# Graph message passing on one core: the last gather of three pairs of groups in four replaced by copied columns of x

## The chip, the cores and the metric

The kernel runs on one core of a Trainium2 chip. The metric is the device time of one execution in microseconds (us). Engines are named as in the profile: PE is the matrix engine (PEld its weight loads), DVE the vector engine, ACT the scalar engine, POOL the general engine that also issues the gathers, SP the engine that issues most of the plain transfers. Each engine runs its own instruction stream in order; streams meet only through semaphores. An engine's sequencer reads the stream, does register work itself and passes the other instructions to the engine.

## The reference

There are 12,500 nodes with 96 features each (x) and 412,500 edges, sorted by their target node. For every edge the reference computes a message, and for every node it sums the messages:

```python
def _mlp(h, W, b, gamma, beta):
    h = relu(h @ W + b)
    mu, var = mean(h, axis=0), mean(square(h - mu), axis=0)
    return gamma * (h - mu) * rsqrt(var + EPS) + beta

node_feat = _mlp(x, W_node, ...)
edge_feat = _mlp(edge_attr, W_edge, ...)            # 4 attributes per edge
message = concatenate([x[row], x[col], edge_feat], axis=1)
message = _mlp(message, W_msg, ...)                 # 288 -> 96
agg = segment_sum(message, col, num_segments=12500)
out = layernorm(x + agg + node_feat)
```

`row` is an edge's source (any node, in no order), `col` its target (sorted). So `x[row] @ W_msg[:96]` needs 412,500 rows from scattered places, and everything that depends on `col` lies in narrow windows.

## The kernel before, in words

The edges are cut into 3223 tiles of 128, four tiles make a group (806 groups), and four groups make a block. The kernel first computes the table `p_tab` = x times the first third of W_msg, and `q_tab` = x times the second third, and writes both to HBM (`tables`). A tile's source rows then come from `p_tab` by one indirect transfer of 128 rows, issued by POOL: `gather` (L207) issues one for each tile of a group, so four for a group. A pair of groups shares a buffer `pg` of [128, 2, 4, 96] floats.

Buffers: `ring` holds 7 such pairs (RING = 14 groups). The first 116 groups (SPILL) are gathered at once while other engines prepare tables and statistics; SP writes them from the ring to HBM (`spill`) and brings them back later (`blocks`, `fetch`, tile `pb`). Three of these groups take their last tile by single rows through SP instead (`EARLY`, `early_rows`). The other 690 groups, the late ones, are gathered during the main loop, `RING` groups ahead: `ahead_of(g)` issues the gathers of group g into the place that group g - RING has left. `plan` mixes early and late blocks into one order of 806 steps.

Before the loop lies a stage with the statistics of nodes (`nodes`) and edges (`edge_norm`). x transposed, [96, 12544], is loaded into the tile `big` (as `xp`) at the start; `nodes` overwrites it with the residual, multiplies that by `center` and stores the result in HBM (`y0_d`). In the loop, from step 64 on, `residual` loads it back into `big`, one part of 8 blocks every fourth step, for the output stage after the loop.

One step of the main loop handles one group. The order on POOL, SP, PE, DVE and ACT is the order of the program (`manual_schedule`). For step k:

- `message(k)`: DVE adds the gathered rows `pg` to the matmul result z and applies relu, giving h (L645).
- `squared` (ACT, every second step, L659) and `moments` (DVE, two adds, L665) for the variance.
- `places_of` (DVE, every fourth step, L653): the 0/1 matrix that sends edges to target nodes.
- `add` (DVE, every fourth step, L708 and L709): adds a block's sums to `agg` at a place that is read from memory into a register (L698).
- `sums(k - 2)` (PE, L689): h times the 0/1 matrix. `edges` (PE, L614) and `prepare` (ACT, L622) make the left operand of a later step.
- `linear(k + 2)` (PE, L628): z, four matmuls of [128 x 128] by [128 x 96].
- for a late group: `ahead_of`, the gathers for the group RING later.

For the groups of the first four blocks (RAW) the rows come from x itself, are transposed on PE and multiplied by W_msg (`transposed`, L633), since `p_tab` is not there yet.

Of the kernel before, what the change touches and what calls it, by code (L numbers as in the profile page):

```python
# [13 lines left out]
F32 = mybir.dt.float32  # L14
BF16 = mybir.dt.bfloat16
I32 = mybir.dt.int32
U8 = mybir.dt.uint8
# [9 lines left out]
P = 128  # L27
# [36 lines left out]
RING = 14  # L64
# [7 lines left out]
CL, CE = 3, 1  # L72
BUSY = 5
# [34 lines left out]
def gnn(ctx, tc, t):  # L108
# [8 lines left out]
    lin_d = dram.tile([len(FETCHED), P], I32, name="lin_d")  # L117
    stack_d = dram.tile([HI + PLACES * BG, RL], BF16, name="stack_d")
# [5 lines left out]
    rpool = ExitStack()  # L124
    nc.sync.dma_start(src_raw, t["src"][:, :RAW * BG * GT])
    ring = rpool.enter_context(tc.tile_pool(name="ring", bufs=RING // 2))
# [90 lines left out]
    def blocks():  # L217

        waiting = []
        for b in range(SPILL // BG + BEHIND):  # L220
            if b < SPILL // BG:
                for i in range(0, BG, 2):
                    pg = ring.tile([P, 2, GT, C], F32, name="pg")
# [45 lines left out]
    with tc.tile_pool(name="win", bufs=1) as win, tc.tile_pool(name="win_ps", bufs=2, space=PSUM) as ps:  # L269
# [8 lines left out]
        nc.sync.dma_start(lin_d, lins)  # L278
        by_block = "p (b g) t -> p b (g t)"
# [202 lines left out]

    order, steps = plan()

    def fast(ring):
        y0s, pair = [], [None]

        def ahead_of(g):
            if g % 2 == 0:
                pair[0] = ring.tile([P, 2, GT, C], F32, name="pg")  # L490
            if g < NG:
                return gather(g, pair[0][:, g % 2, :, :])

        with tc.manual_schedule(engines={ET.SP, ET.Pool}):
# [9 lines left out]
            with tc.tile_pool(name="nd", bufs=1) as nd, tc.tile_pool(name="nd_ps", bufs=2, space=PSUM) as nd_ps, \  # L504
                    tc.tile_pool(name="er", bufs=2) as er, tc.tile_pool(name="es", bufs=2) as es, \
                    tc.tile_pool(name="es1", bufs=1) as es1, tc.tile_pool(name="es_ps", bufs=3, space=PSUM) as es_ps:
                node, n, extra = nodes(nd, nd_ps), 7, early_rows(er)
                for i, _ in enumerate(edge_norm(es, es1, es_ps)):
                    next(node, None)
                    if i:  # L510
                        next(extra, None)
                    while 16 * i + 150 >= 20 * n:
                        next(store, None)
                        n += 1
                for x in (node, store, extra):
                    for _ in x:
                        pass
            got = {g: ahead_of(g) for g in range(SPILL, SPILL + RING)}
        with tc.tile_pool(name="fix", bufs=1) as fix, tc.tile_pool(name="msg", bufs=2) as work, \
# [75 lines left out]

            def transposed(k):
# [27 lines left out]
            def linear(k):  # L624
                s, g = steps[k]
                n = min(GT, NT - g * GT)
                for i in range(n):
# [3 lines left out]
                                     stop=g not in raw)  # L631
# [82 lines left out]
            with tc.manual_schedule(engines={ET.SP, ET.Pool, ET.PE, ET.DVE, ET.Activation}):  # L714
# [13 lines left out]
                for k in range(last):  # L728
# [33 lines left out]
                    if k >= 64 and k % 4 == 0 and loads:  # L762
                        y0s.append(residual(loads.pop(0)))
# [223 lines left out]
    y0s, bad = fast(ring)  # L987
# [5 lines left out]
    rpool.close()  # L993
# [60 lines left out]
```

## Time and profile before

| | |
|---|---|
| time, median of 3 runs | 4123.67 us (4118.46 to 4125.99) |
| profiled execution | 4123.06 us, span 4121.3 us |
| granted PE clock, mean | 0.675 |
| POOL busy | 3092.1 us (75%), of which gathers 3009.5 + 60.8 |
| DVE, ACT busy | 1584.5 us (38%), 1123.0 us (27%) |
| PE, PEld busy | 2632.2 us (64%), 2244.2 us (54%) |

A row of groups in the profile reads: line, engine, operation, what it writes and reads, shapes and count, then busy time in us and the mean duration in ns, then the idle time of the engine right before it and what ended that. A "q" behind an engine's name marks its sequencer. "issue" is time in which the engine waited for nothing that the profile shows.

### The profile page before, as it was taken

To read this page: it belongs to the slowest core of one execution; us is meant where nothing else is said; L and a number is where in the kernel's file an instruction comes from. 1 tells how busy PE (TensorE), PEld (TensorE's weight loads), DVE (VectorE), ACT (ScalarE), POOL (GpSimd) and SP (SyncE) were. 2 spreads that over 40 slices of the span, in tenths; PEclk is the share of its full clock that TensorE was granted. 3 is DMA by queue.
4 is the path that set the end of the run, shared out by engine and by line. 5 is a ranking of instruction groups with operands and counts; after the bars stand their busy time and mean duration, and the time that the engine had idled before them with its cause. 6 is when DMAs were issued, how large, how long until landed. Compare 5 with 4: busy or idle time off the path is not lost.

```text
span 4121.3 us, 43082 instructions
## 1 busy us (share of the span) xinstructions
PE 2632.2 (64%) x14949; PEld 2244.2 (54%) x15169; DVE 1584.5 (38%) x3051; ACT 1123.0 (27%) x1226; POOL 3092.1 (75%) x3248
## 2 busy tenths in 40 slices
PE   4256665666666666666666666666666666666667
PEld 3012324565666656556655566655565565666656
DVE  2499995333333233322333333333233333333323
ACT  1477882222222222212222222222122222222212
POOL 7777777777777777777777777777777777777774
PEclk7667886767766666656667666666666666666665
DMA  8855662223222222222222222222222222222222
GB/s 234 279 140 123 165 161 62 60 70 77 72 50 55 59 57 58 59 54 58 56 58 58 59 47 57 60 58 55 58 59 55 58 60 56 50 59 57 58 45 64
DMA packets 214865, 317.20 MB, mean 77 GB/s; under 512 B 126498, under 2 KB 132988, under 8 KB 211808
## 3 DMA queue, kind: packets, MB, share of 16 engines
q0 software_dynamic: 103040, 158.48, 19.2%
q1 hardware_dynamic: 98635, 150.92, 12.3%
q10 hardware_dynamic: 12960, 4.93, 0.5%
q8 instruction: 122, 2.00, 0.2%
q14 instruction: 108, 0.88, 0.1%
HBM read 258.19 MB, written 55.89 MB: 76 GB/s over the span
## 4 chain that ended last, share of the span: by engine, by line
POOL 50%; issue 22%; DVE 13%; DMA 10%; PE 4%; ACT 1%; SPq 0%; POOLq 0%; another core or an unknown queue 0%; DVEq 0%; ACTq 0%
POOL pg L207 50%; DMA pg<-p_tab,src 9%; DVE estats L419 9%; PE z L628 1%; PE py L971 1%; PE pa L689 1%; DVE mixed L665 1%; DMA x<-in_ea 0%; DVE part L424 0%; DVE h L645 0%; PE pn L358 0%; DVE nstats L360 0%; DVE big L369 0%; DVE y0s L388 0%; DVE agg L394 0%
## 5 line engine op out<-in xcount | busy, mean ns | idle before, releaser
L207 POOL DMA_INDIRECT pg<-p_tab,src x3156 | 3009.5, 954 | 964.7 <-issue 919.7
L628 PE MATMUL z<-rhs,left 128*128 128x96 f32 x6446 | 1276.3, 361 | 1099.9 <-DVE h L645 1092.3
L628 PEld LDWEIGHTS z<-rhs,left 128*128 128x128 f32 x6446 | 1166.7, 267 | 1304.9 <-DVE h L645 1271.9
L645 DVE CUSTOM_DVE_ANT_0 h<-z,pg 128x384 f32<-128x384 f32 x690 | 384.1, 557 | 2301.7 <-DMA pg<-p_tab,src 2244.6
L659 ACT ACTIVATE sq<-h 128x768 f32<-128x768 f32 x404 | 339.8, 841 | 2586.6 <-DVE h L645 2577.5
L689 PE MATMUL pa<-at,h 128*97 128x80 f32 x6446 | 940.5, 307 | 4.9 <-DVE h L645 4.9
L689 PEld LDWEIGHTS pa<-at,h 128*97 128x97 f32 x6446 | 889.4, 227 | 5.9 <-DVE h L645 5.9
L665 DVE TENSOR_TENSOR mixed<-mixed,sq 128x384 f32<-128x384 f32 x802 | 449.8, 561 | 13.9
L622 ACT ACTIVATE left<-pr 127x1024 f32<-127x1024 f32 x403 | 406.8, 1009 | 90.1 <-PE pr L614 60.8
L413 PE MATMUL pr<-ea,wide 128*128 128x512 bf16 x590 | 225.5, 476 | 213.7 <-ACT r L417 135.8
L419 DVE BATCH_NORM_STATS2 estats<-r 128x6 f32<-128x512 f32 x606 | 360.9, 676 | 0.0
L417 ACT ACTIVATE r<-pr 128x1024 f32<-128x1024 f32 x303 | 307.4, 1024 | 93.0 <-DVE estats L419 65.2
L413 PEld LDWEIGHTS <-wide 128*128 128x128 bf16 x606 | 68.8, 114 | 345.9 <-issue 326.1
L614 PE MATMUL pr<-late,we 128*128 128x512 bf16 x515 | 240.6, 530 | 19.2 <-DVE at L653 15.5
L653 DVE TENSOR_TENSOR at<-rel,mixed 128x496 f32<-128x496 bf16 x202 | 135.2, 669 | 6.8
L614 PEld LDWEIGHTS <-we 128*128 128x128 bf16 x806 | 108.4, 144 | 25.2 <-issue 24.7
L207 POOL DMA_INDIRECT pg<-in_x,src_raw x64 | 60.8, 950 | 20.7 <-issue 19.2
L386 PEld LDWEIGHTS pn<-center,big 96*128 96x128 f32 x196 | 42.4, 277 | 33.0 <-DVE y0s L388 22.9
L645 DVE CUSTOM_DVE_ANT_0 h<-z,pb 128x384 f32<-128x384 f32 x100 | 52.5, 548 | 13.6 <-PE z L628 13.5
L386 PE MATMUL pn<-center,big 96*128 96x96 f32 x196 | 41.9, 358 | 17.0 <-DVE y0s L388 16.3
L191 PE MATMUL pt<-w_msg,big 96*128 96x192 f32 x196 | 37.2, 357 | 17.2 <-ACT trow L195 11.7
L709 DVE TENSOR_TENSOR agg<-pa,agg 97x79 f32 x202 | 46.5, 230 | 0.0
(125 smaller groups left out, 658.2 us busy)
## 6 DMA issues: line engine op xcount, KB each, us to landing
pg<-p_tab,src POOLq DMA_INDIRECT x3156
pb<-spill SPq DMA_DIRECT2D x29, 768.0 KB
spill<-pg SPq DMA_DIRECT2D x55, 384.0 KB
ea<-stack_d SPq DMA_DIRECT2D x25, 480.0 KB
stack_d<-y SPq DMA_DIRECT2D x24, 448.0 KB
late<-stack_d SPq DMA_DIRECT2D x57, 180.0 KB
rhs<-q_tab SPq DMA_DIRECT2D x202, 46.5 KB
x<-in_ea SPq DMA_DIRECT2D x8, 896.0 KB
```

The source lines that it names most:

```text
L207: made = [nc.gpsimd.indirect_dma_start(out=pg[:, i, :], out_offset=None, in_=tab[:, :], in_offset=bass.IndirectOffsetOnAxis(ap=idx[:, i:i ...
L413: nc.tensor.matmul(pr[:, k % 2, :], wide[:, P * i:P * (i + 1)], ea[:, b % J, :], start=True, stop=True)
L417: nc.scalar.activation(r, pr, AF.Relu)
L419: nc.vector.bn_stats(stats[:, (k - o) % NS, (k - o) // NS, :], r[:, 1 - o, :])
L614: nc.tensor.matmul(prs[s, half][:, i, :], we[:, 2 * half + i, :], block[s], start=True, stop=True)
L622: nc.scalar.activation(x[:C + WN, 2 * half:2 * half + n, :], pr[:C + WN, :n, :], AF.Relu)
L628: nc.tensor.matmul(zb[k % ZB][:, i * C:(i + 1) * C], left[s % 2][:KR, g % BG, i * P:(i + 1) * P], rhs[:KR, s % RB, g % BG, :], start=True, ...
L645: nc.vector._custom_dve(TENSOR_ADD_SAT, out=h[:, :n, :], in0=z, in1=rows[:, :n, :], s0=MOST, s1=0.0)
L653: nc.vector.tensor_tensor(to, rel[:, b:b + m, :].unsqueeze(3).to_broadcast([P, m, GT, WN]), nodes_of[:, :m].unsqueeze(2).to_broadcast([P, ...
L659: nc.scalar.activation(sq[:, :m, :n, :], hb[k // 2 % HP][:, k % 2:k % 2 + m, :n, :C], AF.Square)
L665: nc.vector.tensor_tensor(wide_sq, wide_sq, sq[:, i, :, :], op=OP.add)
L689: nc.tensor.matmul(by_place[s % 2][:C + 1, :NW], hb[k // 2 % HP][:r, k % 2, t, :], at[s % AB][:r, i, o + NW * t:o + NW * (t + 1)], start=i ...
```

## The change

For 249 pairs of late groups (three pairs in four: `COPIED`) the second group issues three gathers instead of four. Its last tile of 128 edges gets its rows in another way: x transposed stands in `big` during the whole loop, one column for each node, and for each edge of the tile one column (96 partitions, four bytes) is copied into a tile `xc` of [96, 128]. `linear` then multiplies `xc` by the first third of W_msg and adds that to z; the ring's place of that tile is set to zero once, so that `message` adds nothing.

The copies are made by ACT and DVE, in portions of 32: each portion first loads 32 node numbers (times four, as byte addresses) from a small tile into 32 registers of the engine, then issues 32 copies, each from the address in one register. `SHARES` says how many of the 128 columns ACT copies (64, 64, 96 in turn); DVE copies the others. A `Stream` per engine issues at most one portion per step, at most 12 steps ahead of the use, with six `xc` tiles. SP brings the numbers for four pairs at a time (`listed`).

Around it: RING is 16; the ring is eight fixed tiles; x transposed is loaded a second time into `big` near the end of the edge statistics (`back`), after `nodes`, which now advances two steps at a time, has used it; the loads of the residual into `big` move behind the last copy; the scratch for the gathers' descriptors is 8192 instead of the default of 16384 bytes.

```diff
-RING = 14
+RING = 16
+XB = 6
+TURN = 4
+AT_A_TIME = 32
+SHARES = (64, 64, 96)
+AHEAD_BY = 12
+RATE = 0.36
+LP = (NG - SPILL) // 2
+COPIED = [q for q in range(RING // 2, LP - 6) if q % TURN != TURN - 1]
...
+        nc.sync.dma_start(cols, t["lasts"][1::2, :].rearrange("(p k) e -> p k e", k=4))
+        nc.vector.tensor_scalar(cols, cols, 4.0, None, op0=OP.mult)
+        nc.sync.dma_start(col_d.rearrange("(p k) e -> p k e", k=4), cols)
...
+    def back(i):
+        part = slice(i * P, min(i + CH // 2, NB) * P)
+        nc.sync.dma_start(xp[:, part], t["xp"][:, part])
...
         def ahead_of(g):
-            if g % 2 == 0:
-                pair[0] = ring.tile([P, 2, GT, C], F32, name="pg")
+            q = (g - SPILL) // 2
+            slot = ring[q % len(ring)]
+            without = int(g % 2 and q in COPIED)
+            if without and q % len(ring) not in zeroed:
+                zeroed.add(q % len(ring))
+                nc.vector.memset(slot[:, 1, GT - 1, :], 0.0)
             if g < NG:
-                return gather(g, pair[0][:, g % 2, :, :])
+                return gather(g, slot[:, g % 2, :, :], without)
...
+            def columns(j, lo, hi, engine):
+                q = COPIED[j]
+                to = xcs[j % XB].bitcast(U8)
+                _, val = nc.values_load_multi_w_load_instructions(
+                    numbers[q // TURN % 2][:, q % TURN, lo:hi], engines=[engine], min_val=0, max_val=4 * (N - 1),
+                    skip_runtime_bounds_check_because="they are nodes' numbers times four")
+                for i, x in enumerate(val):
+                    a, b = to[:, 4 * (lo + i):4 * (lo + i + 1)], places_in_x[:, bass.ds(x, 4)]
+                    if engine == ET.DVE:
+                        nc.vector.tensor_copy(a, b)
+                    else:
+                        nc.scalar.activation(a, b, AF.Copy)
+
+            class Stream:
+                def __init__(self, engine):
+                    self.engine, self.done, self.due = engine, 0, 0.0
+                    self.parts = [(j, o, o + AT_A_TIME) for j in range(len(COPIED)) for o in range(0, P, AT_A_TIME)
+                                  if (o < SHARES[j % len(SHARES)]) == (engine == ET.Activation)]
+                    self.per = RATE * len(self.parts) / len(COPIED)
+                def step(self, k):
+                    self.due = min(self.due + self.per, 1.5)
+                    while self.due >= 1 and self.done < len(self.parts):
+                        j, lo, hi = self.parts[self.done]
+                        if COPIED[j] // TURN > loaded[-1] or uses[COPIED[j]] - k > AHEAD_BY or \
+                                (j >= XB and uses[COPIED[j - XB]] >= k):
+                            break
+                        columns(j, lo, hi, self.engine)
+                        self.due -= 1
+                        self.done += 1
...
+                    if i == GT - 1 and copied:
+                        nc.tensor.matmul(zb[k % ZB][:, i * C:(i + 1) * C], xcs[COPIED.index(q) % XB],
+                                         w_msg[:, 0, :], start=False, stop=True)
...
-                    if k >= 64 and k % 4 == 0 and loads:
+                    listed()
+                    for x in streams:
+                        x.step(k)
+                    if all(x.done == len(x.parts) for x in streams) and loads:
                         y0s.append(residual(loads.pop(0)))
...
-    nc = bacc.Bacc("TRN2", target_bir_lowering=False, num_devices=1)
+    nc = bacc.Bacc("TRN2", target_bir_lowering=False, num_devices=1, dynamic_dma_scratch_size=8192)
```

More of the change, by code (lines that the diff above doesn't have):

```diff
@@ L123, in gnn @@
     src = const.tile([P, 2, CW], I32, name="src")
-    rpool = ExitStack()
     nc.sync.dma_start(src_raw, t["src"][:, :RAW * BG * GT])
-    ring = rpool.enter_context(tc.tile_pool(name="ring", bufs=RING // 2))
+    ring = [const.tile([P, 2, GT, C], F32, name=f"pg{i}") for i in range(RING // 2)]
     xp = big[:C]
@@ L596, in transposed @@
+            streams = [Stream(e) for e in (ET.Activation, ET.DVE)]
             def transposed(k):
@@ L625, in linear @@
                 s, g = steps[k]
+                q = (g - SPILL) // 2
+                copied = g >= SPILL and g % 2 and q in COPIED
                 n = min(GT, NT - g * GT)
@@ L992, in gnn @@
         output(y0s, "win")
-    rpool.close()
 def kernel(**inputs):
```

38 lines of the change are left out of this document (32 added, 6 removed).

## The prediction, made blind

> **What bounds the kernel now.** I read the page's busy shares and chain of waits first, then the groups, the windows by stage, the timeline of the slowest engine and the waits.
>
> ```profile
> span 4121.3 us, 43082 instructions
> PE 2632.2 (64%) x14949; PEld 2244.2 (54%) x15169; DVE 1584.5 (38%) x3051; ACT 1123.0 (27%) x1226; POOL 3092.1 (75%) x3248
> POOL 50%; issue 22%; DVE 13%; DMA 10%; PE 4%; ACT 1%; SPq 0%; POOLq 0%; another core or an unknown queue 0%; DVEq 0%; ACTq 0%
> L207 POOL DMA_INDIRECT pg<-p_tab,src x3156 | 3009.5, 954 | 964.7 <-issue 919.7
> ```
>
> POOL heads the chain with 50%, and the 22% of "issue" are the pauses between its gathers: 919.7 us over 3156 gathers, 0.29 us each. The timeline shows the beat, and the windows show that it never stops (columns: window, length, then busy us and count for PE, PEld, DVE, ACT, POOL).
>
> ```profile
> 4005.14 0.94 POOL L207 DMA_INDIRECT pg<-p_tab,src  x1 [0.30 <-issue]
> 4006.39 0.95 POOL L207 DMA_INDIRECT pg<-p_tab,src  x1 [0.30 <-issue]
> ...
> 200.00:650.00 450.00, 254.90 (x794) 105.70 (x810) 442.79 (x706) 321.90 (x316) 341.09 (x358) 0.73 0.57 141
> 650.00:2350.00 1700.00, 1131.54 (x7036) 1026.88 (x7142) 528.90 (x1127) 372.33 (x417) 1285.36 (x1361) 0.68 0.27 60
> 2350.00:4057.00 1707.00, 1128.80 (x6654) 1019.22 (x6752) 514.07 (x1097) 350.91 (x397) 1290.77 (x1367) 0.66 0.25 56
> ```
>
> One gather starts every 1.25 us (1700 / 1361 = 1.249, 1707 / 1367 = 1.249; 450 / 358 = 1.257 before the loop). From about 650 us to 4057 us, the loop, the kernel is a line of gathers with everything else waiting for it:
>
> ```profile
> ACT sq L659 <- DVE h L645: 2577.5, 395, 12.4
> DVE h L645 <- DMA pg<-p_tab,src: 2244.6, 617, 8.6
> PE z L628 <- DVE h L645: 1092.3, 470, 7.4
> ```
>
> In those 3407 us DVE is busy for 528.9 + 514.1 = 1043 us and ACT for 372.3 + 350.9 = 723 us. This idle time is what the change spends.
>
> **What the change removes.** `COPIED` holds q from 8 to 338 without every fourth: 249 pairs, one gather less each. 249 x 1.25 = 311 us. In the loop POOL then needs 3407 - 311 = 3096 us. That part is certain; whether anybody can use it depends on who replaces the gathers.
>
> **What it adds.** 249 x 128 = 31,872 copies of one column of x. By `SHARES`, ACT gets 18,592 of them, 581 portions of 32, and DVE 13,280, 415 portions. Each portion is one register load of 32 numbers, and then 32 copies, each with its own address, so a register instruction goes before each. The copies exist nowhere in the trace; their parts do.
>
> The register load has these rows (1 number L715, 8 numbers L572 and L698, 16 numbers L457; min/median/max in ns):
>
> ```profile
> L715 ACTq TENSOR_LOAD <-flag x1: 473/473/473, 641.1 to 641.1; - x1
> L698 DVEq TENSOR_LOAD <-base_at x26: 541/598/612, 678.9 to 4059.2; - x26
> L572 SPq TENSOR_LOAD <-base_at x26: 708/776/806, 655.4 to 3959.9; - x26
> L457 SPq TENSOR_LOAD <-elin x24: 1165/1226/2637, 225.2 to 598.5; - x24
> ```
>
> From 8 to 16 numbers SP's load grows by 450 ns, 56 ns a number. For 24 numbers more than 8 that is 1.35 us: 0.60 + 1.35 = 1.95 us on DVE, 0.47 + 1.35 = 1.8 us on ACT. Ends: 0.5 us if a load of 32 costs what a short one does, 2.45 us at twice the row of 16. I take the middle, since the only step seen between two sizes lies there.
>
> One copy on DVE:
>
> ```profile
> 2153.38 0.16 DVE L708 TENSOR_TENSOR total<-pa,total 97x1 f32<-97x1 f32 x1
> 2153.52 0.24 DVE L709 TENSOR_TENSOR agg<-pa,agg 97x79 f32 x1
> ...
> 2173.36 0.15 DVE L708 TENSOR_TENSOR total<-pa,total 97x1 f32<-97x1 f32 x1
> 2173.43 0.23 DVE L709 TENSOR_TENSOR agg<-pa,agg 97x79 f32 x1
> ...
> L709 DVEq FUSED_REGOPS  x202: 69/69/79, 679.7 to 4063.3; - x101
> L461 SPq MOVE erow<-p_tab x384: 29/29/38, 226.4 to 604.9; - x192
> ```
>
> L709 is the one instruction here with a register for an address. It starts 0.14 us after L708 when the address is worked out between the two (at 2153, behind a load) and 0.07 us when that was done before (at 2173). Its register instruction makes two addresses in 0.069 us; one addition lies nearer the 0.03 of a MOVE. So 0.14 - 0.07 + 0.04 = 0.11 us a copy, between 0.07 and 0.15. A DVE portion: 1.95 + 32 x 0.11 = 5.5 us; 415 of them are 2283 us.
>
> One copy on ACT:
>
> ```profile
> 179.37 1.04 ACT L337 ACTIVATE z<-rlin 128x1024 bf16<-128x1024 f32 x1
> 180.31 1.04 ACT L339 ACTIVATE z<-rlin 128x1024 bf16<-128x1024 f32 x1
> 181.26 1.04 ACT L338 ACTIVATE rlin<-rlin 128x1024 f32<-128x1024 f32 x1
> ...
> L659 ACT ACTIVATE sq<-h 128x768 f32<-128x768 f32 x404 | 339.8, 841 | 2586.6 <-DVE h L645 2577.5 <-DVE h L643 5.5 <-POOL squares L679 3.6
> L310 ACT ACTIVATE y<-x 128x1792 bf16<-128x1792 f32 x8 | 13.5, 1694 | 9.1 <-DVE x L309 8.7 <-DMA x<-in_ea 0.4
> ```
>
> Between 768 and 1792 elements the duration grows by (1694 - 841) / 1024 = 0.83 ns an element, so 201 ns are fixed. Back to back, 1024 elements start every 0.945 us, of which 0.853 are elements: 0.09 us fixed. Four bytes then cost 0.09 to 0.10 us if the next overlaps and 0.20 us if nothing does. The register instruction runs on the sequencer while the engine works on the copy before. I take 0.10. An ACT portion: 1.8 + 32 x 0.10 = 5.0 us; 581 of them are 2905 us.
>
> **What hides what.** A load occupies the sequencer, not the engine, so it can run while the engine works on what was queued before:
>
> ```profile
> L708 DVE TENSOR_TENSOR total<-pa,total 97x1 f32<-97x1 f32 x202 | 30.5, 151 | 4.0 <-PE pa L785 3.0 <-DVE h L645 0.3
> L645 DVE CUSTOM_DVE_ANT_0 h<-z,pg 128x384 f32<-128x384 f32 x690 | 384.1, 557 | 2301.7 <-DMA pg<-p_tab,src 2244.6 <-PE z L628 34.3 <-remote 22.7
> L665 DVE TENSOR_TENSOR mixed<-mixed,sq 128x384 f32<-128x384 f32 x802 | 449.8, 561 | 13.9
> ```
>
> The 26 loads of L698 stand right before L708, and L708 has 4.0 us of idle time in all, not 26 x 0.6. In each step a portion follows h (0.56 us) or the second half of the moments (0.56): 0.5 us of a DVE load is covered, 415 x 0.5 = 208. On ACT it follows sq or left (723 us over about 807 instructions, 0.9 each): 0.85 x 581 = 494. In the loop:
>
> - POOL 3096.
> - DVE 1043 + 2283 - 208 = 3118.
> - ACT 723 + 2905 - 494 = 3134.
>
> Three engines within 40 us of each other. The longest, ACT, saves 3407 - 3134 = 273 us, not 311. Streams that are level also wait for each other: sq waits for h, the moments for sq, h for a gather, and a ring place comes free only after h. The ring of 16 groups holds some 70 us of gathers (16 groups of 3.64 at 1.25 us), so only part is lost; I put 25 us on it, under 1% of the loop.
>
> POOL may itself slow down. A gather that starts while DVE holds both its SBUF inputs is stretched; one that has long started isn't:
>
> ```profile
> 103.15 2.03 DVE L309 TENSOR_TENSOR x<-x,y 128x1792 f32<-128x1792 f32 x1 [7.65 <-ACT y L308]
> 104.04 1.95 POOL L207 DMA_INDIRECT pg<-p_tab,src  x1 [0.30 <-issue]
> ...
> 8.28 0.94 POOL L207 DMA_INDIRECT pg<-in_x,src_raw  x1 [0.30 <-issue]
> 8.79 0.20 DVE L153 TENSOR_SCALAR center<-ident 96x96 f32<-96x96 f32 x1
> ```
>
> The first gather ends 0.82 us after L309 does (105.99 against 105.18), so only the first 0.13 us of a gather needs what DVE held. A copy in flight there costs at most a copy's time. About 2478 gathers are left in the loop; with 0.11 us at most, half of it on average, and DVE copying for 1460 of 3118 us: 2478 x 0.055 x 0.47 = 64 us, and 0 if a copy of four bytes doesn't hold it. With 30 POOL has 3126 us, still level, so it changes nothing in the longest.
>
> On that port the Trainium skill goes further (SBUF — State Buffer, Who interferes with whom): a copy within SBUF may run in a two-port mode, and whoever has the shared pair second is blocked for the whole instruction. L153, a one-source DVE instruction within SBUF, left its gather at 0.94 us, which speaks against a full block; if each copy did block, it is the fifth case below.
>
> **The smaller edits.** The second matmul of each copied tile (249) costs PE 0.36 us by L628's mean, 90 us in all; the 1092 us in which PE waits for h cover it:
>
> ```profile
> L628 PE MATMUL z<-rhs,left 128*128 128x96 f32 x6446 | 1276.3, 361 | 1099.9 <-DVE h L645 1092.3
> big<-in_xp SPq DMA_DIRECT2D x14, 336.0 KB
> big<-y_d SPq DMA_DIRECT2D x12, 384.0 KB
> SPq L578 <- PE z L628: 2914.6, 195, 20.5
> ```
>
> `back` loads xp a second time: 14 loads, 4.8 MB, at the 141 GB/s of the window 200:650 some 34 us of transfers. On SP they pass the edge blocks and the spill stores; POOL doesn't wait there and DVE, 98% busy, sets that stage, so 0, up to 34 if the blocks come late. Running the nodes two steps at a time only moves work within a stage that DVE fills anyway. The residual loads move to the last steps, behind the last copies: 4.8 MB where DMA is a quarter busy. SP has 2915 us of waiting; a late one would hold the output, which reads them in order: 0, up to 10. The list of numbers (2 KB every four pairs) rides on the same SP idle time; if it is late, the register load waits and with it all behind it on ACT and DVE, sq and h first. Ring 16 adds one pair of lead. The descriptor scratch is halved; no row shows a gather waiting for room there (the pauses are a constant 0.30), so 0.
>
> **The sum**, against the profiled execution (4123.06 us for a span of 4121.3; the median of the runs is 0.6 above): 4123 - 273 + 25 + 5 (half of the residual's bound) = 3880 us.
>
> **The rivals.**
>
> - *POOL stays alone the bound* (copies cheaper: a load nearer 1 us or DVE near 0.07). 4123 - 311 = 3812, with the stretch of gathers up to 3850. For it: both copies were priced above their lower ends. Against: the loads have a row at 16 numbers, 1.23 us. Chance 0.27.
> - *The forecast*, three engines level, 3850 to 3960. Chance 0.38.
> - *ACT or DVE dearer by a few per cent*, 3960 to 4115: each 0.005 us on ACT's copy adds 581 x 32 x 0.005 = 93 us. Chance 0.10, and 0.04 for the strip around no change.
> - *Slower: ACT's copies set the pace.* It decides where an ACT portion passes (3407 - 723 + 494) / 581 = 5.47 us, a copy of 0.115. At 0.12 a portion is 5.64, ACT needs 3277 + 229 = 3506, and the time is 4123 + 99 = 4222; at 0.13 it is 4408. For it: the register instruction and the copy share one sequencer, of which no ACT row shows the rate. Against: DVE's rows give 0.11 for both together. Chance 0.16.
> - *Slower: every DVE copy blocks POOL.* 13,280 x 0.07 = 930 us on POOL: 3812 + 930 = 4742. L153 speaks against it. Chance 0.05.
>
> **Range and chances.** 3815 to 4280: below lies little but the bare 3812; above, ACT at 0.123 and more, and the blocked POOL, about 0.15 together. The forecast's own range is 3850 to 3960. Under 0.2% (8 us) a measurement of this kernel cannot tell from no change. Faster 0.27 + 0.38 + 0.10 = 0.75, same 0.04, slower 0.16 + 0.05 = 0.21.
>
> **What would show it.** 2907 gathers from p_tab in place of 3156, plus 64 from x; still 1.25 us apart if POOL keeps its pace, with gaps that end on DVE h where it doesn't. Register loads of 32 near 1.8 to 1.95 us, copies every 0.10 and 0.11 us. ACT's wait for h down from 2577 us, DVE's for pg from 2245, both to a few hundred at most. The forecast is wrong if one of the three engines still waits for a thousand microseconds, or if gathers last beyond 0.95 us throughout.

## The result, and the profile after

The changed kernel takes 4069.51 us in the median (4068.61 to 4070.25), the kernel before, beside it, 4121.07. The ratio is 0.988, with a 95% interval of 0.985 to 0.992: faster by 1.2%, where the prediction said 3880 us, ratio 0.94. Beside each set of runs below the kernel before was timed again, and it takes 4103 to 4121 us in some sets and 5091 to 5199 in others, so each run is compared with the kernel before of its own set.

The page of the changed kernel, its head, the chain of waits and the groups that answer to those shown of before:

```profile
span 4067.6 us, 109367 instructions
PE 2517.9 (62%) x15667; PEld 2155.1 (53%) x15667; DVE 3005.8 (74%) x16338; ACT 2936.1 (72%) x19818; POOL 2853.5 (70%) x2999
...
DVE 28%; issue 24%; ACT 16%; POOL 8%; DMA 7%; DVEq 6%; PE 5%; ACTq 5%; SPq 1%; POOLq 0%
```

```profile
L215 POOL DMA_INDIRECT pg<-p_tab,src x2907 | 2770.4, 953 | 1166.0 <-issue 779.0 <-DVE h L733 250.4 <-DMA spill<-pg 46.8
L653 ACT ACTIVATE xc<-big 96x4 uint8 x18592 | 1863.5, 190 | 589.8 <-issue 569.8 <-PE pr L697 1.7 <-DMA late<-stack_d 1.3
L651 DVE COPY xc<-big 96x4 uint8 x13280 | 1460.9, 196 | 711.2 <-issue 707.5 <-DMA late<-stack_d 2.1
```

POOL led the chain with 50% and now has 8%. Its 2907 gathers still last 0.953 us in the mean, but POOL now stands idle 250 us for h: h frees a ring place, and h is late. DVE and ACT carry the chain, with their loads (DVEq 6%, ACTq 5%). The waits turned round as well:

```profile
POOL pg L215 <- DVE h L733: 250.4, 90, 15.1
ACT sq L747 <- DVE h L733: 151.5, 92, 4.0
DVE h L733 <- PE z L713: 52.7, 23, 7.6
DVE mixed L753 <- ACT sq L747: 51.0, 38, 2.5
```

ACT's wait for h fell from 2577 to 151 us, and DVE's wait for gathers is gone.

Where the time went is read from three rows of each kernel: the edge statistics (the stage before the loop), h (its first start opens the loop) and the gathers (the last start ends it). The columns are min/median/max in ns, then first and last start in us. Before, then after:

```profile
L419 DVE BATCH_NORM_STATS2 estats<-r x606: 633/676/695, 215.4 to 621.5; 128x6 f32<-128x512 f32 x152
L645 DVE CUSTOM_DVE_ANT_0 h<-z,pg x690: 457/557/559, 665.3 to 4059.2; 128x384 f32<-128x384 f32 x173
L207 POOL DMA_INDIRECT pg<-p_tab,src x3156: 940/945/4104, 83.4 to 4056.4; - x198
```

```profile
L431 DVE BATCH_NORM_STATS2 estats<-r x606: 626/676/696, 227.8 to 665.7; 128x6 f32<-128x512 f32 x152
L733 DVE CUSTOM_DVE_ANT_0 h<-z,pg x690: 458/557/561, 709.6 to 4022.0; 128x384 f32<-128x384 f32 x173
L215 POOL DMA_INDIRECT pg<-p_tab,src x2907: 938/944/3408, 84.0 to 4019.2; - x194
```

| part | before, us | after, us | difference |
|---|---|---|---|
| until the first h | 665.3 | 709.6 | +44.3 |
| the loop (first h to the last gather's start) | 3391.1 | 3309.6 | -81.5 |
| from there to the end of the span | 64.9 | 48.4 | -16.5 |
| span | 4121.3 | 4067.6 | -53.7 |

Against the forecast, the loop gave a third of what it was to give, and the stage before it took half of that back.

### The profile page after: what moved, and what is told of

It reads as the page before. It is cut to its first block, busy times and chain, and to the rows that moved or that the text cites. A ratio compares the mean times of both kernels' runs of the same rounds, so it can differ in the third digit from the quotient of the medians.

```text
span 4067.6 us, 109367 instructions
## 1 busy us (share of the span) xinstructions
PE 2517.9 (62%) x15667; PEld 2155.1 (53%) x15667; DVE 3005.8 (74%) x16338; ACT 2936.1 (72%) x19818; POOL 2853.5 (70%) x2999
## 4 chain that ended last, share of the span: by engine, by line
DVE 28%; issue 24%; ACT 16%; POOL 8%; DMA 7%; DVEq 6%; PE 5%; ACTq 5%; SPq 1%; POOLq 0%
ACT xc L653 12%; DVE xc L651 11%; POOL pg L215 8%; DVE estats L431 7%; DVEq L645 6%; ACTq L645 4%; DVE mixed L753 4%; DVE h L733 3%; DMA pg<-p_tab,src 3%; ACT left L705 1%; PE z L713 1%; ACT sq L747 1%; DMA ea<-stack_d 1%; PE pa L777 1%; DMA q_tab<-trow 1%
## 5 line engine op out<-in xcount | busy, mean ns | idle before, releaser
L215 POOL DMA_INDIRECT pg<-p_tab,src x2907 | 2770.4, 953 | 1166.0 <-issue 779.0
L653 ACT ACTIVATE xc<-big 96x4 uint8 x18592 | 1863.5, 190 | 589.8 <-issue 569.8
L651 DVE COPY xc<-big 96x4 uint8 x13280 | 1460.9, 196 | 711.2 <-issue 707.5
L713 PE MATMUL z<-rhs,left 128*128 128x96 f32 x6446 | 1166.5, 340 | 225.6 <-DVE h L733 225.3
L777 PE MATMUL pa<-at,h 128*97 128x80 f32 x6446 | 843.4, 286 | 0.0
L777 PEld LDWEIGHTS pa<-at,h 128*97 128x97 f32 x6446 | 796.6, 206 | 0.2
L697 PE MATMUL pr<-late,we 128*128 128x512 bf16 x690 | 281.7, 501 | 804.3 <-ACT left L705 788.0
L753 DVE TENSOR_TENSOR mixed<-mixed,sq 128x384 f32<-128x384 f32 x802 | 450.3, 561 | 64.9 <-ACT sq L747 51.0
L733 DVE CUSTOM_DVE_ANT_0 h<-z,pg 128x384 f32<-128x384 f32 x690 | 371.0, 553 | 61.5 <-PE z L713 52.7
L718 PE MATMUL z<-w_msg,xc 96*128 96x96 f32 x498 | 125.5, 344 | 0.0
L697 PE MATMUL pr<-early,we 128*128 128x512 bf16 x116 | 46.9, 497 | 115.6 <-ACT left L705 115.4
L718 PEld LDWEIGHTS z<-w_msg,xc 96*128 96x128 f32 x498 | 104.2, 258 | 0.0
```

The costliest lines, as they stand in the source:

```text
L215: made = [nc.gpsimd.indirect_dma_start(out=pg[:, i, :], out_offset=None, in_=tab[:, :], in_offset=bass.IndirectOffsetOnAxis(ap=idx[:, i:i ...
L651: nc.vector.tensor_copy(a, b)
L653: nc.scalar.activation(a, b, AF.Copy)
L697: nc.tensor.matmul(prs[s, half][:, i, :], we[:, 2 * half + i, :], block[s], start=True, stop=True)
L713: nc.tensor.matmul(zb[k % ZB][:, i * C:(i + 1) * C], left[s % 2][:KR, g % BG, i * P:(i + 1) * P], rhs[:KR, s % RB, g % BG, :], start=True, ...
L733: nc.vector._custom_dve(TENSOR_ADD_SAT, out=h[:, :n, :], in0=z, in1=rows[:, :n, :], s0=MOST, s1=0.0)
```

## The experiments

"Loop" below is always the table's second row, from the first start of h to the last start of a gather. The theory under test: in the loop DVE and ACT, each working through its queue in order, are full with copies and the exposed part of their register loads, and wait for each other; POOL starves for ring places; the stage before is a loss of its own. The rival: the loop is held up by something that doesn't depend on the copies' number.

### Fewer copies

```diff
-TURN = 4
-RATE = 0.36
-COPIED = [q for q in range(RING // 2, LP - 6) if q % TURN != TURN - 1]
+TURN = 8
+RATE = 0.3
+COPIED = [q for q in range(RING // 2, LP - 6) if q % TURN in (0, 2, 3, 5, 6)]
```

> Five pairs in eight are copied, always the same places of the ring (TURN 8, RATE 0.3): some 207 pairs for 249; the computation is whole. Theory (DVE and ACT are full in the loop of the changed kernel: 1043 + 2168 = 3211 and 739 + 2433 = 3172 us): DVE needs 1043 + 207 x 8.71 = 2846, ACT 739 + 207 x 9.77 = 2761, POOL 3407 - 207 x 1.25 = 3148 us, so POOL binds with 300 us of room beside it; the loop falls from 3310 to 3150-3180 us and the time to 3910-3940 on a chip on which the changed kernel takes 4069 and the kernel before 4121 (ratio 0.95). Rival (a hold-up of the loop that doesn't come from the copies): 42 more gathers, 52 us more, 4122, ratio 1.00.

Measured: 3906.43 us, ratio 0.948 [0.944, 0.952], a little below the theory's range and far from the rival's 4122. The loop's rows:

```profile
L733 DVE CUSTOM_DVE_ANT_0 h<-z,pg x690: 458/556/560, 711.8 to 3845.7; 128x384 f32<-128x384 f32 x173
L215 POOL DMA_INDIRECT pg<-p_tab,src x2949: 940/945/3587, 83.9 to 3842.9; - x197
```

The loop lasts 3131.1 us, though POOL makes 42 gathers more than in the changed kernel. 3131 is POOL's own need, 3391 - 207 x 1.25 = 3132. Copying less made the kernel 163 us faster than the change does.

### No copies at all, and short loads

```diff
+            for x in xcs:
+                nc.vector.memset(x, 0.0)
...
-                        columns(j, lo, hi, self.engine)
```

> The 31,872 copies and their 996 register loads are left out, on both engines; the buffers hold zeros, so the messages of those tiles lack their column of x. Gathers, second matmuls, lists and the stage before the loop stay as changed. Theory: POOL alone binds the loop, 3096 to 3110 us, with the stage still 44 us late and the tail 16 us short: 4121 - 3392 + 3100 + 44 - 16 = 3857, ratio 0.936; gathers come every 1.25 us through the whole loop. Rival (the loop is held by waits for ring places, lists or matrix products whoever fills the buffers): time within 1% of 4069, ratio 0.98 to 0.99.

Measured: 3854.17 us, ratio 0.937 [0.934, 0.940]. The loop lasts 3078.8 us (709.5 to 3788.3): the whole gain of the removed gathers, 312 us, is there as soon as nobody has to make the copies.

```diff
-                    numbers[q // TURN % 2][:, q % TURN, lo:hi], engines=[engine], min_val=0, max_val=4 * (N - 1),
+                    numbers[q // TURN % 2][:, q % TURN, lo:lo + 1], engines=[engine], min_val=0, max_val=4 * (N - 1),
...
-                for i, x in enumerate(val):
+                for i, x in enumerate(val * (hi - lo)):
```

> Each portion's register load brings one number instead of 32, and all 32 copies use it, so the copied columns are wrong; the copies, their number and their address instructions stay. In the changed kernel the loads of 32 take 2.10 us on DVE and 1.97 on ACT, of which 707.5 and 569.8 us are exposed. With one number a load takes some 0.5 us, less than the 0.56 or 0.84 us of the instruction before it. Theory: DVE needs 1043 + 1461 + about 80 = 2580, ACT 739 + 1863 + about 60 = 2660, POOL 3096 us binds; loop about 3110-3140, time 3870-3900, ratio 0.94 to 0.95. Rival (the copies themselves, not the loads, hold the loop): time above 4000.

Measured: 3853.16 us, ratio 0.935 [0.932, 0.939], below the theory's 3870 to 3900; the loop 3079.4 us (704.8 to 3784.2). With all 31,872 copies made, this is the time without any. The loads in the changed kernel, then here:

```profile
L645 ACTq TENSOR_LOAD <-numbers x581: 1952/1967/1979, 714.3 to 3985.0; - x194
L645 DVEq TENSOR_LOAD <-numbers x415: 2096/2101/2145, 715.5 to 3975.0; - x139
```

```profile
L645 ACTq TENSOR_LOAD <-numbers x581: 275/279/289, 710.8 to 3688.2; - x194
L645 DVEq TENSOR_LOAD <-numbers x415: 301/306/333, 712.0 to 3681.6; - x139
```

Ahead of the copies themselves, in the page's groups of the run with short loads:

```profile
L653 ACT ACTIVATE xc<-big 96x4 uint8 x18592 | 1824.3, 193 | 0.0
L651 DVE COPY xc<-big 96x4 uint8 x13280 | 1425.4, 197 | 54.9 <-issue 52.0
```

A short load of 0.3 us hides behind the instruction before it, wholly on ACT and nearly on DVE: the idle time ahead of ACT's copies falls from 590 us to 0, of DVE's from 711 to 55. With the copies but without the exposed loads DVE needs 1043 + 1425 + 55 = 2523 us and ACT 739 + 1824 = 2563 (739 is its other work in the loop, sq and left), both below POOL's 3079. It takes the exposed loads to lift the two streams above POOL.

### One stream at a time

```diff
-                        columns(j, lo, hi, self.engine)
+                        if self.engine == ET.Activation:
+                            columns(j, lo, hi, self.engine)
```

and the same with `ET.DVE`; the buffers start as zeros in both.

> DVE's 13,280 copies and 415 loads are left out, ACT's stay as changed; the columns that DVE copied are zeros. ACT's own need in the loop is 739 + 1863.5 + 569.8 = 3172 us, above POOL's 3096, and DVE has 2168 us of room. Theory (each stream costs its own work, and the 98 us by which the loop of 3310 lies above DVE's 3212 are the two in-order queues waiting for each other): the loop lasts 3172 to 3190 us, time 3930-3950, ratio 0.955. If ACT alone loses as much by waiting as the two together, the loop lasts 3270 and the time is 4030.

Measured: 3901.47 us, ratio 0.950 [0.947, 0.953]; the loop 3139.9 us (707.9 to 3847.8), 32 us below the 3172 worked out for ACT, and so below the theory's range.

> ACT's 18,592 copies and 581 loads are left out, DVE's stay; the columns that ACT copied are zeros. DVE's own need in the loop is 1043 + 1460.9 + 707.5 = 3211 us. Theory (as in the run with ACT's copies only): the loop lasts 3211 to 3230 us, time 3970-3990, ratio 0.965, later than with ACT's copies alone; both lie 80 to 130 us below the changed kernel, which has both. Rival (the ring of 16 and the order of the steps hold DVE up, whatever ACT does): the loop stays at 3300 and the time within 15 us of 4069.

Measured: 3975.72 us, ratio 0.968 [0.965, 0.971]; the loop 3200.7 us (708.1 to 3908.8), against 3211 worked out for DVE. The rival, a loop of 3300 us whatever ACT does, is out: without ACT's copies the loop falls by 109 us.

So POOL alone needs 3079, ACT alone 3140, DVE alone 3201, and together they take 3310. The 109 us above the longest exist only with both streams. Most of them stand in DVE's own waits. In the changed kernel, by the waits shown with the result, DVE stands 52.7 us at h for z, which is made from ACT's `left`, and 51.0 us at the moments for ACT's sq. With DVE's copies alone the page has:

```profile
L756 DVE TENSOR_TENSOR mixed<-mixed,sq 128x384 f32<-128x384 f32 x802 | 449.6, 561 | 13.9
L736 DVE CUSTOM_DVE_ANT_0 h<-z,pg 128x384 f32<-128x384 f32 x690 | 369.0, 552 | 27.6 <-PE z L716 18.2
```

That is 104 us for the two waits with both streams and 18 with one. The copied columns themselves are in time for their use: h waits 3.5 us in all for the products that read them (L718). The timeline of the changed kernel shows one of the places where the two queues hold each other up:

```profile
2002.64 0.56 DVE L733 CUSTOM_DVE_ANT_0 h<-z,pg 128x384 f32<-128x384 f32 x1
2002.83 2.57 ACT L653 ACTIVATE xc<-big 96x4 uint8 x26
...
2004.93 3.14 DVE L651 COPY xc<-big 96x4 uint8 x29 [1.73 <-issue]
...
2008.36 0.38 DVE L651 COPY xc<-big 96x4 uint8 x3 [0.29 <-issue]
2008.70 0.56 DVE L733 CUSTOM_DVE_ANT_0 h<-z,pg 128x384 f32<-128x384 f32 x1
...
2009.36 0.84 ACT L747 ACTIVATE sq<-h 128x768 f32<-128x768 f32 x1 [3.96 <-DVE h L733]
```

DVE has a portion queued between two h: its load (1.73 us exposed) and its 32 copies. ACT is through with its own portion at 2005.4 and stands 3.96 us at sq, which needs the second h; its next portion stands behind sq. With 3201 and 3140 of 3310 us taken, DVE and ACT have little slack to make that up.

### The stage before the loop

```diff
-                    for _ in range(2):
-                        next(node, None)
+                    next(node, None)
                     if i:
                         next(extra, None)
-                    if i > 14:
-                        for _ in range(min(3, len(homes))):
-                            back(homes.pop(0))
```

The first run has both edits, the second only the lower one (the loads of xp all at the end).

> The changed kernel with three pairs in four, single node steps and the second loads of xp all at the end of the stage; the computation is whole. With five pairs in eight the same edit brought the first h from 711.8 to 677.1 us and the time down by 41 us; there POOL was the bound. Theory (the in-order streams of DVE and ACT start earlier too, so the shift comes through): first h near 677, time 4069 - 30 to -40 = 4030-4040, ratio 0.977 to 0.981. Rival (streams that wait for each other absorb it): above 4060.

Measured: 4037.93 us, ratio 0.983 [0.980, 0.986]; first h at 675.4, the loop 3306.3 us.

> Double node steps as in the changed kernel, only the second loads of xp at the end of the stage; the computation is whole. In the changed kernel SP's queue waits 60.9 + 15.1 us at the y0 stores of line 389, which the double steps bring in a lump, and edge blocks (37.0 us on PE) and spill stores (42.2 us on POOL) queue behind them. Theory (the y0 stores in a lump cost the stage its 44 us): first h still near 710 us or later, time 4060-4085. Rival (the loads of xp among the edge blocks cost it): first h near 677, time 4030-4040.

Measured: 4062.76 us, ratio 0.989 [0.986, 0.992]; first h at 703.2, the loop 3307.3 us. The statistics of the first, then of the second:

```profile
L431 DVE BATCH_NORM_STATS2 estats<-r x606: 633/675/695, 225.5 to 631.6; 128x6 f32<-128x512 f32 x152
```

```profile
L431 DVE BATCH_NORM_STATS2 estats<-r x606: 630/675/695, 227.2 to 659.4; 128x6 f32<-128x512 f32 x152
```

From first to last start the stage takes 406.1 us before, 437.9 after, 406.1 with both edits and 432.2 with the loads alone moved. So 26 us are the doubled node steps, 6 the loads of xp. The other 12 lie earlier, where the statistics start (215.4 before, 227.8 after): DVE waits 8.4 us there for the list of all columns' numbers, the rest of that wasn't traced further. In the changed kernel's waits between 200 and 715 us the doubled steps look so:

```profile
SPq L389 <- DVE y0s L400: 60.9, 7, 10.8
SPq L389 <- DVE pick L440: 15.1, 1, 15.1
```

```profile
PE pr L425 <- DMA ea<-stack_d: 37.0, 7, 9.8
POOL pg L215 <- DMA spill<-pg: 42.2, 5, 22.8
```

SP's queue stands at the y0 stores (line 389) until DVE has made their contents, and the edge blocks (`ea`) and spill stores that follow on the same queue come late. With single steps there is no wait at line 389 left, and POOL's wait for spill stores is 12.5 us.

### Both together

> Five pairs in eight as in the run before the two others, and the stage before the loop as it was in the kernel before: single node steps, the second loads of xp all at the end of the stage; the computation is whole. Theory: the edge statistics end near 622 instead of 666 us and, POOL being the bound, POOL's stalls of that stage (46.8 us on spill stores in the changed kernel) go too: 35 to 45 us less than with five in eight alone, 3870-3900, ratio 0.94. Rival (the loads at the end make the first copies late, and the loop gives the time back): within 10 us of five in eight alone.

Measured: 3865.08 us, ratio 0.939 [0.935, 0.943]: 41 us less than five in eight alone. It beats both kernels, and is the prediction's time within 15 us; that is chance, since it has 42 copied pairs fewer.

### Where the kernel before takes 5100 us

Eight runs fell in sets where the kernel before takes 5091 to 5199 us: two in three (TURN 3, RATE 0.32), one in two (TURN 2, RATE 0.24), the two edits of the stage, twice the lead (XB 12, AHEAD_BY 24) and portions of 16 numbers (AT_A_TIME 16, the due count's cap 3.0), these last two kernels twice. Where the expectations speak of chips, read sets: the record numbers the chips of these sets 4, 5 and 9, but 4 and 5 are also the numbers of the sets at 4103 and 4120 us. Whether the chip makes the difference is therefore not shown.

> Two pairs in three are copied (221 instead of 249; TURN 3, RATE 0.32); the computation is whole. In the profile of the changed kernel the copies and the exposed part of their register loads cost ACT 1863.5 + 569.8 = 2433 us (9.77 us a pair) and DVE 1460.9 + 707.5 = 2168 us (8.71 us a pair), on top of 739 and 1043 us of other work. Theory (DVE and ACT, each working through its queue in order, are full in the loop and POOL starves for a ring place): with 221 pairs DVE needs 1043 + 1925 = 2968, ACT 739 + 2159 = 2898, POOL 3407 - 221 x 1.25 = 3131 us; POOL binds again, the loop falls from 3310 to 3131-3180 us, the time to 3890-3940. Rival (something else holds the loop up by a fixed amount, the matrix products or waits for ring places): 28 more gathers cost 35 us and the time rises to about 4105.

> One pair in two is copied (166; TURN 2, RATE 0.24); the computation is whole. Theory: DVE needs 1043 + 166 x 8.71 = 2489, ACT 739 + 166 x 9.77 = 2361, POOL 3407 - 166 x 1.25 = 3200 us. POOL binds with nothing near it; its loop lasts 3200 to 3220 us, and with the 44 us by which the loop starts later than before the time is 3940-3980, slower than with two pairs in three by about 69 us. Rival (a fixed hold-up): 83 more gathers than in the changed kernel, 4069 + 104 = 4173, slower than before.

> The stage before the loop as it was: one step of the node work for each step of the edge work, and all 14 second loads of xp at the end of the stage, not spread over it; the computation is whole. In the changed kernel the edge statistics end at 666.4 us instead of 622.1, 44 us late. Theory A (the doubled node steps and the loads among the edge blocks disturb that stage, and the loop, bound by itself, starts 44 us late): the statistics end again near 622 us and the time falls by 35 to 45 us, to 4025-4035. Theory B (the loop's in-order streams absorb a shift of their start, or the loads at the end now hold the first copies up): the statistics end earlier, but the time falls by under 10 us.

> Only the 14 second loads of xp move to the end of the stage; the node work still goes two steps at a time; the computation is whole. If the loads (4.8 MB on SP's queue ahead of edge blocks and spill stores) cause the late statistics, they end near 622 us here as in the variant with single node steps. If the doubled node steps do (their DVE and ACT work and y0 stores come in one lump), they stay near 666 us and the time stays within 10 us of the changed kernel's 4069.

> XB 12 for 6 and AHEAD_BY 24 for 12: twice the buffers for copied columns and twice the steps by which a copy may run ahead of its use; the computation is whole. Theory (the 108 us come from h, sq, moments and left, which stand in order behind the portions on the two queues; where the copied columns go doesn't matter): loop 3290-3320, time 4050-4080, the wait of sq for h near 150 us as in the changed kernel. Rival (portions are held back by the lead and the buffers, and come in bunches): the loop falls towards DVE's 3202, time 3960-4010.

> AT_A_TIME 16 for 32, and room for more than one portion in a step (the cap of the due count 3.0 for 1.5): the same 31,872 copies behind 1992 loads of 16 numbers; the computation is whole. A load of 16 took 1.23 us on SP before the change, against 2.10 and 1.97 us for 32 here. Theory (a load is exposed by its length less the instruction that runs meanwhile): DVE 830 x (1.23 - 0.5) = 606 us exposed for 707, ACT 1162 x (1.1 - 0.8) = 350 for 570; DVE needs 3110, ACT 2950, the loop 3180-3250, time 3940-4010. Rival (twice the loads, and most of the added ones find only a copy of 0.1 us to hide behind): exposed 830 x 1.0 and 1162 x 0.9, loop above 3350, time above 4100.

> XB 12 for 6 and AHEAD_BY 24 for 12, as in the run with twice the lead; the computation is whole. On a chip on which the kernel before takes about 4110 us: theory (in-order queues wait for each other at h, sq, moments and left, whatever lead the columns have): loop 3290-3320 us, time 4050-4080. Rival (too few buffers and too little lead): the loop falls towards 3202, time 3960-4010.

> AT_A_TIME 16 for 32 with the due count's cap at 3.0, as in the run with portions of 16; the computation is whole. On a chip on which the kernel before takes about 4110 us: theory (exposed is a load's length less the instruction that runs meanwhile): loop 3180-3250 us, time 3940-4010. Rival (most of the added loads find only a copy to hide behind): loop above 3350, time above 4100. On the other chip the ratio rose from 1.112-1.115 to 1.145, which speaks for the rival.

One thing in the first expectation is not so: eight pairs share the ring's places in turn, and with two in three a copied pair can meet a gathered pair's old rows there, so its sums hold rows too many. The instructions are those described.

| run | copied pairs | us | ratio, 95% interval |
|---|---|---|---|
| one in two | 166 | 5526.72 | 1.063 [1.061, 1.065] |
| two in three | 221 | 5643.02 | 1.085 [1.083, 1.088] |
| single node steps | 249 | 5783.3 | 1.112 [1.108, 1.115] |
| loads late | 249 | 5795.0 | 1.115 [1.113, 1.117] |
| twice the lead | 249 | 5686.6, 5688.35 | 1.117 [1.114, 1.120], 1.115 [1.113, 1.118] |
| portions of 16 | 249 | 5829.01, 5833.3 | 1.145 [1.142, 1.148], 1.144 [1.142, 1.147] |

None of the times expected for the first four applies there. Their order still speaks against a fixed hold-up: more copies, more time. To see what is different there, the two kernels themselves were run without an edit:

> The kernel before, no edit. On a chip on which it takes some 5100 us: if late instructions are the cause, its gathers still last 0.945 us but start more than 1.25 us apart, with 'issue' ahead of instructions on PE, DVE and ACT; if slow memory is the cause, gathers and transfers last longer. On the other chip: 4110 us and the profile already shown.

> The changed kernel, no edit. On a chip on which the kernel before takes some 5100 us: copies wait for their instructions, so the ratio lies with those of the runs with three pairs in four there, 1.11 to 1.12. On the other chip: 4069 us, ratio 0.985 to 0.992, first h at 710 us, loop 3310.

Both fell in such a set: the kernel before 5067.91 us in its one run, the changed kernel 5694.63, ratio 1.116 [1.113, 1.118]. There the change is a loss of 12%. The kernel before there, by its groups and then its waits; the last fence is one wait of the same kernel at 4121 us:

```profile
L207 POOL DMA_INDIRECT pg<-p_tab,src x3156 | 3007.9, 953 | 1866.3 <-issue 897.2
L628 PE MATMUL z<-rhs,left 128*128 128x96 f32 x6446 | 1212.4, 321 | 761.7 <-issue 758.8
L689 PE MATMUL pa<-at,h 128*97 128x80 f32 x6446 | 1000.3, 286 | 965.5 <-issue 963.0
```

```profile
POOL pg L207 <- DVE h L645: 755.7, 139, 19.6
```

```profile
PE z L628 <- issue: 2.5, 5, 1.7
```

A gather (953 ns) and a product (321 ns for 361) last no longer than at 4121 us. What is new is that PE stands for 759 and 963 us ahead of the products of `z` and `pa` with nothing to wait for that the profile shows, where it was 2.5 us ahead of `z`. POOL then waits for h. DVE's and ACT's longest waits there, 2343.7 us ahead of h and 2104.3 ahead of `left`, are put down to "remote", an unknown queue, so the profile does not say what ended them. PE's weight loads and products in such a stretch:

```profile
2000.09 0.24 PEld L689 LDWEIGHTS pa<-at,h 128*97 128x97 f32 x1 [0.46 <-issue]
2000.79 0.29 PE L689 MATMUL pa<-at,h 128*97 128x80 f32 x1 [0.95 <-issue]
...
2001.49 0.29 PE L689 MATMUL pa<-at,h 128*97 128x80 f32 x1 [0.41 <-issue]
```

In the changed kernel the same happens to the copies (their address instructions by line, then ACT's timeline):

```profile
L653 ACTq ALU_OP  x18592: 2/35/1458, 983.3 to 5600.2; - x200
```

```profile
2039.80 0.20 ACT L653 ACTIVATE xc<-big 96x4 uint8 x1 [0.53 <-issue]
2040.49 0.20 ACT L653 ACTIVATE xc<-big 96x4 uint8 x1 [0.49 <-issue]
2041.22 0.20 ACT L653 ACTIVATE xc<-big 96x4 uint8 x1 [0.52 <-issue]
...
2050.53 3.15 ACT L653 ACTIVATE xc<-big 96x4 uint8 x32 [1.03 <-issue]
```

In some stretches a copy comes every 0.7 us, in others 32 of them in 3.15 us, 0.095 us apart as at 4068 us. An address instruction takes up to 1458 ns there, with the same median of 35. Over the run ACT's idle time ahead of copies is 1797 us instead of 590. The beat of 0.7 us is common to several engines. Counting starts 0.67 to 0.73 us after the start before on the same engine, the traces have 480 on PE in the kernel before here and 15 at 4121 us; in the changed kernel 729 on ACT, 684 on DVE and 192 on SP here, and 31, 30 and 4 at 4068 us. So here instructions start late, whichever kernel runs, at one beat for several engines, and a change that trades 249 gathers for 31,872 copies, each with an instruction for its address, pays for it. What sets the beat no run shows.

Twice the lead changes nothing there (1.115 to 1.117 beside 1.116); portions of 16 cost 3% more. Whether the lead or smaller portions would move the 109 us where the kernel before takes 4121 us is open: both kernels came to the other sets twice.

## Why the prediction was wrong, point by point

The direction and the mechanism held: gathers give way to copies, and DVE, ACT and POOL end within 4% of each other (3201, 3140 and 3079 us). The size did not: -53.7 us of span for a forecast of -243.

- *POOL*: 3096 us were put on it, 3079 measured without copies. The 16 us between are that the forecast took 3407 us for the loop of before, where first h to last gather are 3391. Right.
- *The copies*: 0.11 and 0.10 us each; the timeline has 32 of ACT's in 3.15 us and the groups sum to 1461 us for 13,280 on DVE and 1864 for 18,592 on ACT, 0.110 and 0.100. Right.
- *ACT*: 3134 put, 3140 measured alone. Right, with some luck: by the measured rows the parts add up to 3172. The load was put at 1.8 us by adding the step from 8 to 32 numbers to a row of one number; 31 steps of 56 ns would have given 2.2, and it takes 1.97.
- *DVE*: 3118 put, 3201 measured alone, so DVE and not ACT is the longest. The copies and the 1043 us of other work stood, and the mis-sized term is the exposed loads: 601 us forecast (415 x 1.95 less 208 hidden), 707.5 measured. A load takes 2.10 us, 63 us more in all, and hides 0.40 us, (872 - 707.5) / 415, and not 0.5.
- *"I put 25 us on it, under 1% of the loop"*: the failed step that cost most. The level streams lose 109 us to each other (3310 with both, 3201 with DVE's alone). The forecast compared the streams with the ring, which holds 70 us of gathers, and overlooked that DVE and ACT have no such store between them: h, sq and the moments hand over from portion to portion.
- *The stage before the loop, "only moves work within a stage that DVE fills anyway"*: failed, 44 us for 0. The work moved within DVE's stage, but its y0 stores moved on SP's queue too, ahead of the edge blocks and spill stores. 26 us are the doubled steps, 6 the loads of xp (the bound of 34 was right in kind and high), 12 the later start, in which the list of numbers has 8.4.
- *The end*: 5 us later were put for the residual loads; it is 16.5 us shorter. The 196 products of the output take 275 ns each instead of 421, and the granted clock from the last gather on is 0.88 where it was 0.51. With five in eight, POOL-bound again, it is 0.50 and the end takes 65 us. Why the clock differs was not tested. Without the change, too, an execution can be that much shorter (some take 4101 to 4103 us, others 4118 to 4126), so this gain need not be the change's. The windows of before and after from the last gather on (window, length, busy us and counts, then the clock):

```profile
4057.00:4121.00 64.00, 49.86 (x220) 47.47 (x218) 28.25 (x56) 14.92 (x28) 21.18 (x22) 0.51 0.30 79
```

```profile
4020.00:4067.60 47.60, 31.66 (x267) 30.32 (x265) 29.05 (x62) 15.57 (x30) 20.90 (x22) 0.88 0.40 106
```

- *The second products*: 90 us were put on PE, for 249 instructions. The profile counts two records for each product of this kind, 498, and 125.5 us; PE had no idle time ahead of them (L718), so nothing follows from it.

The sum closes: 248 forecast for the loop, less 16 for its length, 67 for the longest stream (3201 for 3134) and 84 for the waiting (109 for 25), leaves 81; less 44 and plus 16.5, that is 53.7 before rounding.

Of the rivals, the result lies in the one that priced a stream dearer by a few per cent, 3960 to 4115, and in part by its mechanism: DVE's stream is dearer by 83 us, through its loads and not its copies. That alone would have left the time near 3947 us (3880 + 67), inside the forecast's own range; the waiting and the stage before the loop carried it out. The two slower ones are out: they do not explain the sets at 5100 us either, where copies and gathers last as long. ACT's copy is 0.100 us, not 0.115. And DVE's copies do not block POOL: the gather's median is 944 ns where it was 945, and in the short-load run, with all copies made, the loop is as long as without copies. By the Trainium skill (SBUF — State Buffer, Who interferes with whom) a DVE copy in its two-port mode that issues first would shut POOL out for its whole length; these copies show nothing of that on POOL's side. On DVE's side the two do meet: the copies last 155 to 429 ns with a median of 169, and of the 2806 over 200 ns in the trace of the changed kernel 2373 start 0.50 to 0.80 us after the start of a gather and 423 start 1.20 to 1.25 us after one. It hardly costs a beat: the next copy starts 106 ns later in the median, after long copies and short ones.

## What to carry to other kernels

When work moves from one bound engine to two that have room, do not fill all three to the same level: engines that hand work to each other in order need slack, and five pairs in eight beat six in eight by 163 us. Price a register load as an instruction that stops its sequencer, with about the one instruction before it as cover (0.40 us of 2.10 on DVE behind 0.56, 0.99 of 1.97 on ACT behind 0.83 to 1.00), and count for every moved step its DMAs on the queue they join. And a kernel that gets faster by many tiny instructions leans on how fast instructions can start: time it on several occasions, each beside the kernel before.

## What the hardware showed that was not expected

- The same kernel takes 4121 us in one set of runs and 5100 in another, 24% more, with equal durations of gathers, copies and vector work; the difference shows as waiting ahead of instructions that wait for nothing in the profile, on PE in the kernel before, on ACT and DVE in the changed one, in stretches with a beat of 0.70 us. The Trainium skill (Runtime: NRT & Kernel Launch, Instruction fetch mechanics) has it that fetching is hidden because the sequencer dispatches more slowly than its store is filled. The run at 4068 us agrees, with copies 0.095 us apart; at 5692 us the rows show instructions 0.7 us apart in stretches, and if that is fetching, it is not hidden there. Two things speak against fetching: the common beat, and the instruction packets of 8 KB, which take 0.44 us in the median of the trace at 4068 us and 0.43 at 5692.
- A register load costs by the number: 0.28 us (ACT) and 0.31 us (DVE) for one, 1.97 and 2.10 for 32, so 54 and 58 ns for each further number in the mean.
- The granted clock of the last 50 to 64 us, 0.88 or 0.50, goes with an end that is 16 us shorter or longer. Runs in which ACT's stream was full had the high one (0.86 with single node steps, 0.89 with ACT's copies alone); short loads, no copies and DVE's copies alone had the low one (0.50 to 0.53). The cause is open.
